# Layer 0's attention in 64-token chunks: a two-layer kernel on one core

## Chip, cores and metric

The kernel runs on one core of one Trainium2 chip, in one launch. The metric is the device time of an execution in microseconds (us); the median of several runs is compared. TensorE (PE in the profile) multiplies matrices into PSUM, with weight loads (PEld) beside it; VectorE (DVE), ScalarE (ACT) and GpSimd (POOL) work on elements; SyncE (SP) issues most DMAs.

## What is computed

The input is 16 sequences of 512 tokens with 128 features. Two layers follow, each as x + attention(norm(x)) + feed-forward(norm(x)). Cut to what matters:

```python
x  = L0_attn_x                                   # (16, 512, 128), float32
xn = layernorm(x)
x  = x + linear_attention(xn) + moe(xn)          # layer 0
xn = layernorm(x)
x  = x + softmax_attention_64(xn) + channel_mix(xn)   # layer 1

def linear_attention(x):                         # 16 heads of 8
    q, k, v = heads(x @ Wq.T), heads(x @ Wk.T), heads(x @ Wv.T)
    q, k = rope(q, k); q, k = elu(q) + 1, elu(k) + 1
    for each token t:                            # per head
        K_sum += k_t ; KV += outer(k_t, v_t)
        y_t = (q_t @ KV) / max(q_t . K_sum, 1e-6)
    return y @ Wo.T
```

`moe` sends each token to the 2 best of 8 experts (hidden size 512, squared ReLU) and adds a shared expert. Layer 1's softmax attention lets a query see all keys up to the end of its chunk of 64.

The change touches `linear_attention` alone. It is computed in chunks: the tokens of earlier chunks enter through a running state (KV and K_sum summed over them), those of the query's own chunk through masked scores, (q k^T where key <= query) times v. A column of ones beside v gives the denominators.

## The kernel before

**Recorder and scheduler.** The code records its operations instead of issuing them. `Program.call` (line 314) keeps each with an engine, an estimated cost and its tiles; for TensorE it also keeps a form, the rows and columns of the array that are used. `program.unit()` groups matmuls that are issued without a break. `Program.run` (line 409) then goes through them as a list scheduler: for each engine it takes, of what is ready, what was recorded first, and it emits every instruction. So all instructions carry the lines of the emitting helpers (L326; L331 for whole matmuls split into four strips of 32 columns, so that the array's shape stays; L514 for matmuls with constants that fill planned pauses of more than `IDLE`). One reads the profile by tiles. `TURN` (line 278) is what the scheduler reckons for a change of shape. Indirect DMAs on POOL are kept `SPACE` apart and tied to a matmul of that time.

**What sets the recorded order.** Four chains of generators: `dispatch` (norm, routing, sending tokens to their experts' slots by indirect DMAs), `slot_tiles` (the experts), `layer0`, `layer1`. The sequences form four groups of four; layer 0 of a group is recorded beside layer 1 of the group before. `PACE` (line 284) gives each chain its begin and its pace, one row for the first group, one for the middle ones, one for the last; `LAYER_STEPS` (line 108) is the number of steps for a sequence.

**Layer 0's attention**, for a sequence of NT = 4 tiles of P = 128 tokens:

- `linear_operands` (line 964) projects q, k, v, applies rope and phi (tile `qr`), and writes v into strips (`vpad`, `vstrips`). Then come the states: for each of the first three tiles a matmul of `qr` with `vstrips` adds to one accumulator in PSUM, and VectorE copies it, masked by head blocks (`blocks`), into a state tile. Each copy stands between two matmuls of the same accumulator. Then q and k are transposed to `qT`, `kT`, and ScalarE makes `q0m`: q four times, each with other heads zeroed.
- `linear_attention` (line 1055) goes through the tiles t. `scores(t)` is a unit of 8 matmuls (32 rows by 128 columns of the array, 256 moving columns) into two pairs of PSUM banks; VectorE masks both pairs with `causal` into `am` (two products of 128x1024). `weigh(t, ams, oT)` (line 1086) is a unit of 8 matmuls that read the state (`q0T,state`, from the second tile on) and 16 with the masked scores (`am,vpad`), all 128 rows by 32 columns with 128 moving columns, into one bank. ScalarE copies it to `oT`. After two tiles `finish` transposes back and divides.

Layer 1 shows in the profile as `qa,ka` (scores for maxima), `maxima` (VectorE), `ka,qa` (scores again, transposed), `ex` (ScalarE's exponential) and `ex,vpad` (weighted values).

Of the kernel before, what the change touches and what calls it, by code (L numbers as in the profile page):

```python
# [29 lines left out]
F32 = mybir.dt.float32  # L30
# [24 lines left out]
def slot_count(gt):  # L55
# [14 lines left out]

VPAD = (H - 1) * (PAIR + 2) + 32
# [17 lines left out]
    ("causal", P), ("rank", E), ("upper", P), ("ones", P), ("tile", SLOT_TILES),  # L89
# [18 lines left out]
LAYER_STEPS = (16, 40)  # L108
# [145 lines left out]
class Op:  # L254


    def __init__(self, engine, emit, cost, later, index):
        self.engine, self.emit, self.cost, self.later, self.index = engine, emit, cost, later, index
        self.needs, self.bases, self.wrote, self.then = set(), set(), set(), []
        self.missing, self.ready, self.result, self.done = 0, 0.0, None, False  # L260

        self.spaced = False

        self.form, self.strips, self.narrow = None, None, False
# [13 lines left out]
TURN = {(32, 128): 208, (128, 32): 138, (128, 128): 148}  # L278

SPACE = 1900  # L280

# [3 lines left out]
    (0.1, 0.4, 0.26, 0.8, 0.0, 0.8, 0.0, 1.23),  # L285
    (0.3, 0.4, 0.2, 0.8, -0.09, 1.0, 0.22, 1.0),
    (0.0, 0.58, 0.27, 0.76, 0.18, 1.0, 0.0, 1.0),
# [3 lines left out]
class Program:  # L291
# [22 lines left out]
    def call(self, name, api, method, args, kw):  # L314
# [18 lines left out]
        if name == "PE":  # L333
# [4 lines left out]
            elif args[1].shape[0] == 32:  # L338
                cost = max(0.425 * n, 56.0)
            elif o.shape[0] == 32:  # L340
                cost = max(0.425 * n, 56.0)
            else:
                cost = max(1.68 * n, 224.0)
# [16 lines left out]
        if name == "PE":  # L360
            (self.unit_of[0] if self.unit_of else op).form = form
# [47 lines left out]
    def run(self):  # L409
# [20 lines left out]
        while emitted < len(self.ops):  # L430
# [27 lines left out]
            if op.spaced:  # L458
                self.spaced_to = start + SPACE
# [6 lines left out]
            if name == "PE":  # L466
                if self.form != (P, P) and all(part.strips for part in op.parts or [op]):
                    op.form, op.narrow = (P, 32), True
                if op.form != self.form:
                    end += TURN.get(op.form, 148)  # L470
                    self.form = op.form
# [152 lines left out]
def two_layers(ctx: ExitStack, tc: tile.TileContext, x, small, const, w_fc, w_proj, out):  # L624
# [145 lines left out]
    for i in range(NT - 1):  # L770
        st = fixed.tile([P, 8, 32], F32, tag=f"state{i}", name=f"state{i}")
# [158 lines left out]
    def tokens_to_heads(o, name, tag):  # L930
# [11 lines left out]
        "vpad": 0, "qr": ("qr", 1), "T": ("q0T", "k0T", 1), "q0m": ("q0m", 2), "am": ("am", 2),  # L942
# [3 lines left out]
        "vpad": 2, "qr": ("ka", 2), "T": ("qa", "qa", 2), "q0m": ("probs", 4), "am": ("ka", 2),  # L946
# [3 lines left out]

    def lent_layer():

        a = p3.tile([P, 1024], F32, tag="probs", name="vstrips_lent", bufs=4)
        LENT["vstrips"] = a[:, 0 : NT * 8 * (PAIR + 2)].rearrange(
            "p (t s e) -> p t s e", t=NT, e=PAIR + 2
        )
        G.memset(a, 1.0)
        a = p3.tile([P, 1024], F32, tag="probs", name="states_lent", bufs=4)
        LENT["states"] = [
            a[:, i * 256 : (i + 1) * 256].rearrange("p (s e) -> p s e", e=32) for i in range(NT - 1)  # L960
        ]
        G.memset(a, 0.0)

    def linear_operands(xnT, b, home):
# [51 lines left out]
        pst = one(f"state_{b}")  # L1016
        for t in range(NT - 1):
            M.matmul(
                pst[:, 0 : 8 * (PAIR + 2)], qr[:, t, D : 2 * D],
                vs[:, t, :, :].rearrange("p s e -> p (s e)"),  # L1020
                start=(t == 0), stop=(t == NT - 2), skip_group_check=True,
            )
            V.tensor_tensor(
                states[t][:, :, 0 : PAIR + 2],
                pst[:, 0 : 8 * (PAIR + 2)].rearrange("p (s e) -> p s e", e=PAIR + 2), blocks,
                ALU.mult,
            )
# [13 lines left out]
        qT, kT = both  # L1041
        qms = []
        for u in range(2):
            tag, bufs = home["q0m"]
            qm = (p3 if tag == "probs" else p2).tile(
                [P, 2, T], F32, tag=tag, name=f"q0m_{b}_{u}", bufs=bufs
            )
            for o in range(2):
                r = 2 * u + o
                S.activation(qm[:, o, :], qT, AF.Copy, scale=c_("pick")[:, r : r + 1])  # L1050
            qms.append(qm)
# [3 lines left out]
    def linear_attention(operands, b, home):  # L1055
# [4 lines left out]
        def scores(t):  # L1060

            scs = [big(f"sc0_{b}_{t}_{pr}") for pr in range(2)]
            cols = slice(t * P, (t + 1) * P)
            with program.unit():
                for u in range(2):
                    for j in range(4):
                        rows = slice(32 * j, 32 * j + 32)
                        M.matmul(
                            scs[j // 2][:, j % 2, 2 * u * P : 2 * (u + 1) * P].rearrange(
                                "p (o q) -> p o q", o=2  # L1070
                            ),
                            kT[rows, cols], qms[u][rows, :, cols], start=True, stop=True,
                        )
            ams = []
            for pr, sc in enumerate(scs):
                tag, bufs = home["am"]
                am = p2.tile([P, 2, 512], F32, tag=tag, name=f"am_{b}_{t}_{pr}", bufs=bufs)
                V.tensor_tensor(
                    am.rearrange("p j (t q) -> p j t q", q=P),
                    sc.rearrange("p j (t q) -> p j t q", q=P),  # L1080
                    causal.unsqueeze(1).unsqueeze(1).to_broadcast([P, 2, NT, P]), ALU.mult,
# [4 lines left out]
        def weigh(t, ams, oT):  # L1086

            po = one(f"o0_{b}_{t}")

            with program.unit():  # L1090
                for u in range(2):
                    for j in range(4):
                        o = po[32 * j : 32 * j + 32, u * P : (u + 1) * P]
# [765 lines left out]
```

## Time and profile before

| | |
|---|---|
| runs shown | 1570.34, 1570.38, 1571.56 us, median 1570.38 |
| profiled execution | 1572.36 us; its span from first to last instruction 1570.6 us |
| granted TensorE clock | 0.997 |
| matmul records of TensorE | 23232 |
| layer 1's `maxima`, VectorE | 448 instructions, 385.7 us |
| layer 1's `ex`, ScalarE | 320 instructions, 311.5 us |
| layer 0's mask `am`, VectorE | 128 instructions, 151.0 us |
| layer 0's copies to `oTs`, ScalarE | 64 instructions of 128x256, 24.0 us |

A group's row reads: line, engine, operation, out<-in, shape, count, then busy time, mean duration of one in ns, and idle time of the engine just before, with what ended it. "32*128" ahead of a shape is the part of the array: rows by columns. Durations of matmuls overlap, so their sum is not time; the distance from one start to the next is. A row of the timeline reads: start, length from the first start to the last end, engine, line, operation, shape, count, and in brackets idle time before it.

### The profile page before, as it was taken

What the parts mean: (1) busy time and instruction counts of PE and PEld (TensorE: products, weight loads), DVE (VectorE), ACT (ScalarE), POOL (GpSimd) and SP (SyncE); (2) the same over time, 40 slices, a digit from 0 to 9 for tenths busy, and PEclk for the clock granted to TensorE, in tenths of its full rate; (3) what the DMA queues carried; (4) which work ended last, traced back from release to release, by engine and by line L of the source; (5) the groups of instructions that cost most, each with busy time, mean ns of one, the idle gap of its engine ahead of it and who ended that gap; (6) DMA issues with size and microseconds to landing.
All of it is one profiled execution on the core that took longest, in us unless ns stands there. A gap on an engine that the chain in (4) does not pass through costs nothing. (4 is left out here: it accounts for less than half of the span.)

```text
span 1570.6 us, 53937 instructions
## 1 busy us (share of the span) xinstructions
PE 1474.0 (94%) x23232; PEld 977.6 (62%) x23232; DVE 1064.1 (68%) x2289; ACT 865.0 (55%) x1369; POOL 392.3 (25%) x425
## 2 busy tenths in 40 slices
PE   6899998999999999999999999999999989998887
PEld 5678887766666657666666666566666555444444
DVE  6864431787876777588685767586757786765763
ACT  3336464565655555655656566655665545455444
POOL 3540142342035241114400140200000521442220
PEclk9999999999999999999999999999999999999999
DMA  6247687554244554334241434431321100000000
GB/s 191 89 132 233 188 245 224 161 159 146 83 141 128 146 145 133 99 110 137 83 136 36 141 98 124 119 89 53 108 85 42 39 27 15 22 15 8 8 2 14
DMA packets 150238, 163.09 MB, mean 104 GB/s; under 512 B 12912, under 2 KB 97648, under 8 KB 150000
## 3 DMA queue, kind: packets, MB, share of 16 engines
q1 hardware_dynamic: 141808, 142.86, 30.8%
q0 software_dynamic: 8192, 16.79, 3.6%
q8 instruction: 182, 2.98, 0.8%
q14 instruction: 56, 0.46, 0.1%
HBM read 118.71 MB, written 40.89 MB: 102 GB/s over the span
## 5 line engine op out<-in xcount | busy, mean ns | idle before, releaser
L326 DVE TENSOR_REDUCE maxima<-banks 128x2 f32<-128x768 f32 (+2 forms) x448 | 385.7, 914 | 82.1 <-PE banks L326 77.2
L326 ACT ACTIVATE ex<-banks 128x1024 f32<-128x1024 f32 x320 | 311.5, 1021 | 137.7 <-PE banks L326 130.1
L326 DVE TENSOR_TENSOR am<-banks,const_sb 128x1024 f32<-128x1024 f32 x128 | 151.0, 1220 | 122.1 <-PE banks L326 118.3
L326 PE MATMUL banks<-qa,ka 32*128 32x512 f32 (+3 forms) x2048 | 194.1, 460 | 14.5 <-ACT ex L326 6.3
L1223 POOL DMA_INDIRECT rows<-xn,pl_slot x128 | 128.1, 1000 | 304.5 <-DVE pl_slot L326 173.4
L326 PE MATMUL banks<-ka,qa 32*128 32x512 f32 (+2 forms) x1792 | 185.0, 503 | 17.5 <-ACT ex L326 10.9
L1242 POOL DMA_INDIRECT back<-results,pl_slot x128 | 128.1, 1001 | 290.2 <-PE banks L326 184.0
L326 PE MATMUL banks<-ex,vpad 128*32 128x512 f32 (+3 forms) x2048 | 173.1, 439 | 0.9 <-issue 0.5
L326 PEld LDWEIGHTS banks<-qa,ka 32*128 32x128 f32 x2048 | 95.8, 183 | 91.3 <-ACT ex L326 25.6
L326 ACT ACTIVATE hg<-banks 128x512 f32<-128x512 f32 x156 | 92.9, 597 | 103.6 <-PE banks L331 80.1
L326 PEld LDWEIGHTS banks<-ka,qa 32*128 32x128 f32 x1792 | 80.4, 184 | 79.5 <-issue 20.1
L331 PE MATMUL banks<-wp,hg 128*32 128x128 f32 x3104 | 104.9, 274 | 10.2 <-issue 6.0
L326 PEld LDWEIGHTS banks<-ex,vpad 128*32 128x32 f32 x2048 | 52.6, 109 | 91.4 <-issue 64.3
L331 PE MATMUL banks<-xgT,wf 128*32 128x128 f32 x3104 | 106.0, 274 | 3.3 <-issue 1.6
L331 PEld LDWEIGHTS banks<-wp,hg 128*32 128x32 f32 x3104 | 87.5, 110 | 34.5 <-issue 21.1
L331 PEld LDWEIGHTS banks<-xgT,wf 128*32 128x32 f32 x3104 | 85.9, 110 | 27.6 <-issue 11.5
L326 ACT COPY oTs<-banks 128x256 f32<-128x256 f32 (+1 forms) x96 | 42.8, 445 | 98.7 <-PE banks L326 93.8
L326 PE MATMUL banks<-am,vpad 128*32 128x128 f32 x2048 | 82.2, 274 | 4.5 <-issue 2.0
L326 ACT ACTIVATE hg<-hg 128x1024 f32<-128x1024 f32 x80 | 83.0, 1038 | 2.5
L326 PE MATMUL banks<-q0m,k0T 32*128 32x256 f32 x1024 | 74.6, 400 | 2.3 <-ACT ex L326 1.0
L326 ACT COPY yg<-banks 128x256 f32<-128x256 f32 x80 | 29.3, 367 | 83.6 <-PE banks L331 60.4
L326 PEld LDWEIGHTS banks<-am,vpad 128*32 128x32 f32 x2048 | 59.2, 110 | 15.5 <-issue 8.3
(226 smaller groups left out, 2343.9 us busy)
## 6 DMA issues: line engine op xcount, KB each, us to landing
wf<-in_w_fc SPq DMA_DIRECT2D x156, 256.0 KB
wp<-in_w_proj SPq DMA_DIRECT2D x156, 256.0 KB
rows<-zeros SPq DMA_DIRECT2D x4, 2496.0 KB
results<-yg SPq DMA_DIRECT2D x76, 128.0 KB
xg<-rows SPq DMA_DIRECT2D x36, 256.0 KB
x_in<-in_x SPq DMA_DIRECT2D x16, 256.0 KB
x<-x SPq DMA_DIRECT2D x16, 256.0 KB
out<-rr SPq DMA_DIRECT2D x16, 256.0 KB
```

The lines of the kernel that those rows point to most:

```text
L326: return getattr(api, method)(*map(made, args), **{k: made(a) for k, a in kw.items()})
L331: yield api.matmul(to[at : at + 32], weights[:, at : at + 32], *rest, **kw)
L1223: i = nc.gpsimd.indirect_dma_start(out=rows.made()[:, :], out_offset=bass.IndirectOffsetOnAxis(ap=slot.made(), axis=0), in_=row.made(), in ...
L1242: "POOL", lambda: nc.gpsimd.indirect_dma_start(out=o.made(), out_offset=None, in_=results.made()[:, :], in_offset=bass.IndirectOffsetOnAxi ...
```

## The change

Chunks become CH = 64 tokens, so there are eight chunks and seven states. The steps now go by pairs of tiles (tp), two for a sequence. `scores(tp)` is one unit of 16 matmuls (32 rows by 64 columns, 256 moving columns; for the one sequence with borrowed buffers 32 of 128), two masks instead of four for a pair. `weigh(tp)` is one unit: 24 or 32 state reads (32 by 32) and 64 products with masked scores (64 by 32), all of 64 moving columns, into two banks, and one ScalarE copy. The states come from one unit of seven matmuls (64 rows), two masked copies, and six sums on VectorE. `LAYER_STEPS`, `PACE` and the scheduler's estimates of costs and turns change with it. The constants `SPACE_FIRST` and `SPACE` are equal.

```diff
+CH = P // 2
+CHUNKS = T // CH
+STATE_N = 8 * (PAIR + 2) + 16
...
-    ("causal", P), ("rank", E), ("upper", P), ("ones", P), ("tile", SLOT_TILES),
+    ("causal", CH), ("rank", E), ("upper", P), ("ones", P), ("tile", SLOT_TILES),
...
-LAYER_STEPS = (16, 40)
+LAYER_STEPS = (12, 40)
...
-TURN = {(32, 128): 208, (128, 32): 138, (128, 128): 148}
+TURN = {(32, 128): 208, (32, CH): 208, (128, 32): 138, (CH, 32): 138, (128, 128): 148}
+SPACE_FIRST = 1900
...
-    (0.1, 0.4, 0.26, 0.8, 0.0, 0.8, 0.0, 1.23),
-    (0.3, 0.4, 0.2, 0.8, -0.09, 1.0, 0.22, 1.0),
-    (0.0, 0.58, 0.27, 0.76, 0.18, 1.0, 0.0, 1.0),
+    (0.1, 0.4, 0.31, 0.68, 0.0, 0.58, 0.01, 1.28),
+    (0.3, 0.41, 0.12, 0.8, -0.26, 1.0, 0.25, 1.0),
+    (-0.27, 0.45, 0.41, 0.66, 0.05, 0.94, 0.2, 0.89),
...
-            elif args[1].shape[0] == 32:
-                cost = max(0.425 * n, 56.0)
-            elif o.shape[0] == 32:
-                cost = max(0.425 * n, 56.0)
+            elif form[0] == CH and form[1] == P:
+                cost = 0.84 * n
+            elif form[0] == 32 and form[1] > 32:
+                cost = max(0.425 * n * o.shape[0] / P, 28.0)
+            elif form[1] == 32:
+                cost = max(0.425 * n, 28.0)
...
-        pst = one(f"state_{b}")
-        for t in range(NT - 1):
-            M.matmul(
-                pst[:, 0 : 8 * (PAIR + 2)], qr[:, t, D : 2 * D],
-                vs[:, t, :, :].rearrange("p s e -> p (s e)"),
-                start=(t == 0), stop=(t == NT - 2), skip_group_check=True,
-            )
-            V.tensor_tensor(
-                states[t][:, :, 0 : PAIR + 2],
-                pst[:, 0 : 8 * (PAIR + 2)].rearrange("p (s e) -> p s e", e=PAIR + 2), blocks,
-                ALU.mult,
-            )
+        n = 8 * (PAIR + 2)
+        pst, last = big(f"state_{b}"), one(f"state_last_{b}")
+        with program.unit():
+            for i in range(CHUNKS - 1):
+                t, c = i // 2, i % 2
+                rows = slice(c * CH, (c + 1) * CH)
+                M.matmul(
+                    pst[:, c, t * n : (t + 1) * n] if i < CHUNKS - 2 else last[:, 0:n],
+                    qr[rows, t, D : 2 * D], vs[rows, t, :, :].rearrange("p s e -> p (s e)"),
+                    start=True, stop=True, skip_group_check=True,
+                )
+        V.tensor_tensor(
+            states[0][:, :, 0:n].rearrange("p (t c) e -> p c t e", c=2),
+            pst[:, :, 0 : 3 * n].rearrange("p c (t e) -> p c t e", t=3),
+            c_("blocks").unsqueeze(1).unsqueeze(1).to_broadcast([P, 2, 3, n]), ALU.mult,
+        )
+        V.tensor_tensor(states[1][:, 0, 0:n], last[:, 0:n], c_("blocks"), ALU.mult)
+        for i in range(1, CHUNKS - 1):
+            upto = state_of(states, i)[:, 0:n]
+            V.tensor_tensor(upto, upto, state_of(states, i - 1)[:, 0:n], ALU.add)
...
+        def parts(tp):
+            for t in (2 * tp, 2 * tp + 1):
+                for c in range(2):
+                    yield t, c, slice(c * CH, (c + 1) * CH), slice(t * P + c * CH, t * P + (c + 1) * CH)
...
-        def scores(t):
+        def scores(tp):
...
+                for r, n, qm in qms:
+                    for t, c, half, cols in parts(tp):
+                        at = (t % 2) * 4 * CH + r * CH
+                        for j in range(4):
+                            rows = slice(32 * j, 32 * j + 32)
+                            M.matmul(
+                                scs[j // 2][half, j % 2, at : at + n * CH].rearrange(
+                                    "p (o q) -> p o q", q=CH
+                                ),
+                                kT[rows, cols], qm[rows, :, cols], start=True, stop=True,
+                            )
...
-        def weigh(t, ams, oT):
-            po = one(f"o0_{b}_{t}")
+        def weigh(tp, ams, oT):
+            po, begun = big(f"o0_{b}_{tp}"), set()
...
+                for t, c, _, cols in parts(tp):
+                    for u in range(2):
+                        for j in range(4):
+                            if 2 * t + c:
+                                o, kw = to(t, c, u, j)
+                                at = (4 * u + j) * (PAIR + 2)
+                                rows = slice(32 * j, 32 * j + 32)
+                                M.matmul(
+                                    o, state_of(states, 2 * t + c - 1)[rows, at : at + 32],
+                                    qT[rows, cols], stop=False, **kw,
+                                )
+                for t in (2 * tp, 2 * tp + 1):
+                    for u in range(2):
+                        for o_ in range(2):
+                            for j in range(4):
+                                for c in range(2):
+                                    half = slice(c * CH, (c + 1) * CH)
+                                    o, kw = to(t, c, u, j)
+                                    at = (t % 2) * 4 * CH + (2 * u + o_) * CH
+                                    M.matmul(
+                                        o, strip(vp, t, 8 * u + 2 * j + o_)[half, :],
+                                        ams[j // 2][half, j % 2, at : at + CH],
+                                        stop=(o_ == 1), **kw,
+                                    )
-            S.copy(oT[:, (t % 2) * 2 * P : (t % 2 + 1) * 2 * P], po[:, 0 : 2 * P])
+            S.copy(
+                oT.rearrange("p (n c q) -> p n c q", c=2, q=CH),
+                po[:, :, 0 : 4 * CH].rearrange("p c (n q) -> p c n q", q=CH),
+            )
...
-        i.spaced = True
+        i.spaced = SPACE_FIRST if sent is not None and len(rows_in) == 0 and not routed else SPACE
```

`to(t, c, u, j)` is the place of the result: partitions 32j to 32j+31 of bank c, 64 columns at (2 (t mod 2) + u) 64.

## The prediction

> **What bounds the kernel now.** I read four views: the page's busy times, the busy times by stretch, the groups of instructions, and the timeline of TensorE. First the page and three stretches. I cut them where the trace shows layer 1's first product with the probabilities (`ex,vpad`, 328 us) and layer 0's last product with the masked scores (`am,vpad`, 1335 us).
>
> ```profile
> PE 1474.0 (94%) x23232; PEld 977.6 (62%) x23232; DVE 1064.1 (68%) x2289; ACT 865.0 (55%) x1369; POOL 392.3 (25%) x425
> 0.00:328.00 328.00, 295.63 (x4549) 236.19 (x4549) 179.29 (x467) 159.76 (x292) 107.45 (x133) 0.99 0.60 180
> 328.00:1335.00 1007.00, 975.49 (x16360) 633.05 (x16363) 735.92 (x1524) 592.21 (x929) 219.49 (x239) 1.00 0.34 101
> 1335.00:1571.00 236.00, 202.92 (x2331) 108.34 (x2322) 148.88 (x300) 113.01 (x150) 65.33 (x55) 0.99 0.04 11
> ```
>
> After the length come PE, PEld, DVE, ACT and POOL, then granted clock, DMA share and GB/s. In the 1007 us in the middle TensorE is busy 97% of the time at full clock, VectorE 73%, the DMA engines a third. So in the stretch that holds most of layer 0, TensorE's stream sets the time, and what it no longer streams is gained. The last 236 us are layer 1 alone.
>
> Next the groups that the change touches, then TensorE's timeline, where durations overlap and only distances between starts are a price.
>
> ```profile
> L326 PE MATMUL banks<-am,vpad 128*32 128x128 f32 x2048 | 82.2, 274 | 4.5 <-issue 2.0 <-DVE am L326 1.6 <-DVE maxima L326 0.5
> L326 PE MATMUL banks<-q0m,k0T 32*128 32x256 f32 x1024 | 74.6, 400 | 2.3 <-ACT ex L326 1.0 <-issue 0.6 <-DVE maxima L326 0.6
> L326 DVE TENSOR_TENSOR am<-banks,const_sb 128x1024 f32<-128x1024 f32 x128 | 151.0, 1220 | 122.1 <-PE banks L326 118.3 <-ACT ex L326 2.6 <-ACT h L326 0.8
> L326 DVE TENSOR_TENSOR state<-banks,const_sb 128x144 f32<-128x144 f32 x45 | 13.7, 304 | 20.2 <-PE banks L326 15.3 <-PE banks L331 3.1 <-issue 1.0
> L326 DVE TENSOR_TENSOR pl_sum<-pl_sum 128x128 f32<-128x128 f32 x16 | 4.7, 291 | 0.5
> ```
> ```profile
> 67.96 0.40 PE L326 MATMUL banks<-q0T,state 128*32 128x128 f32 x8
> 68.18 0.42 PE L326 MATMUL banks<-am,vpad 128*32 128x128 f32 x6
> 68.92 0.43 PE L326 MATMUL banks<-am,vpad 128*32 128x128 f32 x5 [0.32 <-issue]
> 69.68 0.44 PE L326 MATMUL banks<-am,vpad 128*32 128x128 f32 x5 [0.32 <-issue]
> 70.04 1.15 PE L326 MATMUL banks<-q0m,k0T 32*128 32x256 f32 x16
> ...
> 616.85 0.46 PE L331 MATMUL banks<-small_sb,xnT 128*32 128x8 f32 x32
> 617.24 1.14 PE L326 MATMUL banks<-qa,ka 32*128 32x512 f32 x8
> ...
> 709.22 0.40 PE L326 MATMUL banks<-q0T,state 128*32 128x128 f32 x8
> 709.43 0.62 PE L326 MATMUL banks<-am,vpad 128*32 128x128 f32 x16
> ...
> 747.74 1.15 PE L326 MATMUL banks<-q0m,k0T 32*128 32x256 f32 x16
> 748.82 1.07 PE L326 MATMUL banks<-ex,vpad 128*32 128x256 f32 x16
> ```
>
> `128*32` is the part of the array used: 128 rows (the contraction) by 32 columns. A float32 matmul has two records (1024 `am,vpad` matmuls are built, 2048 recorded). From 709.22 to 709.43, eight records of 128 columns on four tiles side by side take 0.218 us, by neighbouring starts too: a pass of 128 columns is 109 ns, shared by four tiles. From 747.74 to 748.82, sixteen records of 256 columns take 1.08 us: 0.87 of stream at that rate and 0.21 for changing the array's shape. The 32 records of 8 columns at 616.85 are not streaming but issue: 0.46 us less one duration of 0.18 us, so a start each 8.8 ns, its weight load included. At 68.18 the sixteen records that should take 0.44 us take 1.86: an "issue" stall, 1.4 us lost. TensorE's waits list 45 gaps of this kind, 16.3 us.
>
> **The change, part by part.** The built order gives the counts: 12,078 matmuls before, 13,387 after. All prices are 109 ns a pass of 128 columns, two passes a matmul, divided by the tiles side by side.
>
> Removed, all 16 sequences. Scores: 512 matmuls of 256 columns on four tiles, 109 ns each, 55.8 us. Products with the masked scores: 1024 of 128 columns, 54.5 ns, 55.8. State reads: 384, 20.9. State updates: 22 whole ones of 144 columns at 245 ns and 104 strips at 61, 11.8. Together 144.3 us.
>
> Added. Scores: 480 of 256 columns and 64 of 128, on 32x64 tiles, eight of which fit the array: 54.5 and 27 ns, 27.9 us. State updates: 112 of 144 columns, two side by side, 122.6 ns, 13.7. State reads: 896 of 64 columns on four diagonal 32x32 tiles, 27.2 ns, 24.4. Masked products: 2048 of 64 columns on 64x32 tiles. No row shows eight tiles in this form. The low end is streaming, 54.5 ns for a pass of eight, 27.9 us; the high end is only four at once, 55.8. I take issue as the limit, since the 8-column burst is the nearest row: 8 x 8.8 = 70 ns for a pass of eight, 35.8 us. Together 101.8, a gain of 42.5.
>
> Changes of shape: 838 before, 841 after, hence nothing (0.8 us from the different mix, counted at 0.21 us into a shape of 32 rows and 0.14 to 0.15 into the others). Elsewhere, other products stand whole or in strips in another mix and there are ten more filling matmuls: +2.1. TensorE's stream: -42.5 + 0.8 + 2.1 = -40 us.
>
> [...]
>
> VectorE: masks go from 128 to 64 of the same size, 64 x 1.22 = -78 us. States: 48 x 0.304 = 14.6 removed; added for each sequence one product of 864 elements (1.05 us, between 0.691 for 512 and 1.22 for 1024), one of 144 (0.30) and six sums (0.29 each, by `pl_sum`), 3.1 x 16 = 50. Net -43 us. On an engine at 73% beside TensorE at 97% this is hidden; it pays only where TensorE waited for it (`am` 2.7 us, `maxima` 14.8): -3. The six sums stand in line before the first read of a state, 2.7 us after the update; the scores and two masks (2.4 us) are ahead of that read anyway, and if uncovered it costs at most 1 us for each sequence, as other units are ready. ScalarE: 64 copies at 0.375 become 32 at 0.587, -5 us, hidden. SP's queue has as many entries as before, POOL one memset less; the spacing of POOL's indirect DMAs keeps its 1900, so their queues only follow TensorE.
>
> Order. The begins and paces are new, and the built order shows their effect: before layer 1's first `ex,vpad` stand six sequences' masked products (five before), and after layer 0's last there are 5.4 sequences' `ex,vpad` (4.25 before). So 1.1 sequences more of layer 1 run alone. Pricing the built streams as above, the tail had 192 us of stream in 236 us, 44 lost on 4.25 sequences, 10.4 each: +12. The middle had 943 of stream in 1007, 6.8% lost; it now has some 90 us less stream: -6. Together +6.
>
> Stalls at issue. Each weighing unit now has 88 or 96 short matmuls, with loads 352 or 384 instructions, as fast as 4.4 ns each; 64 in a row is the longest such burst that the trace has. Of the 64 old weighing units 4 stalled (seven of the gaps stand before an `am,vpad`); with four times the density I take one in four of the 32 new ones, 8 x 1.4 = +11 (ends: none, and all, +45).
>
> Sum: -40 - 3 + 6 + 11 = -26 us. The profiled span is 1570.6 (its run's own time 1572.4); the median of the runs is 1570.38, the span within 0.02%, so I take the difference off it: **1544 us**.
>
> **Rivals.** First, the two halves of the rows do not run together in the masked products. For it: no row has both row and column parts. Against: row parts alone (`q0m,k0T`) and column parts alone (`am,vpad`) each run four at once. Price +20, with some 6 us less of stalls: 1558.
> Second, no stalls at all and streaming the limit: 8 off the stream and 11 off the stalls, 1525. For it: six of the eight 8-column bursts ran through.
> Third, slower: instruction supply becomes the bound of the weighing units. The longer runs of narrow products never went faster than 16 instructions in 218 ns, 13.6 ns each. If TensorE cannot be fed faster for long, the 2944 short matmuls, 11,776 instructions, take 160 us in place of 60: 1544 - 11 + 100 = 1633. It decides from 8.2 ns an instruction, where 97 us would eat up the 37 that remain without stalls. Two of the eight bursts, which broke off after 22 and 26 records, speak for it; that the old runs were paced by their columns speaks against.
> Fourth, the change is made but the order gives all back, no change: a middle bound by layer 1's own chain. The 86 us a sequence in the middle (1007 over 11.75) against 55 alone (236 over 4.25) speaks against.
>
> **How the numbers follow.** Forecast 0.40, second 0.24, first 0.22, slower 0.10, no change 0.04. A measurement of this kernel can tell some 0.2% from nothing. All but the last two are faster: 0.86, 0.04, 0.10. Range: from below the second case (1525, its order term uncertain by one sequence, 10 us) to above the first (1558, the same): 1517 to 1567. The slower case stays outside.
>
> **What would show it.** In the changed profile: starts of `am,vpad` some 9 ns apart in eights with 55 to 70 ns from one eight to the next (right), or in fours with 55 (first rival); `q0m,k0T` units of 16 matmuls in about 1.1 us; the masks 64 times at 1.22; "issue" before TensorE below 35 us; `ex,vpad` alone for some 290 us at the end. Wrong: weighing units beyond 3 us, or TensorE's idle in the middle up by more than 30 us.

## The result, and the profile after

The changed kernel is slower: 1596.88 us in the median (1591.32 to 1599.50, four runs) against 1570.36 for the kernel before on the same chip, a ratio of 1.0159 [1.0141, 1.0177]. The profiled span went from 1570.6 to 1597.7 us, +27.1. (In the diff above, the `oT` side of ScalarE's copy should read `p (n c q) -> p c n q`, like the side of `po` below it.)

The busy times of the page, and the instruction queue among its DMA queues:

```profile
PE 1462.7 (92%) x25850; PEld 966.3 (60%) x25850; DVE 1024.4 (64%) x2305; ACT 857.1 (54%) x1337; POOL 387.9 (24%) x424
q8 instruction: 203, 3.33, 0.9%
```

TensorE is less busy than before by 11 us and yet the span is longer. Its instructions arrived in 203 packets of 16,384 bytes (182 before). 25,850 matmul records and as many weight loads over 203 packets are 255 instructions a packet (255 before too), so I take a packet for a block of 256 instructions; in `f4` below they come 256 at a time. A float32 matmul, with two records and two loads, is four instructions.

The busy times by stretch, cut at the same two events as before (first `ex,vpad`, now at 376 us; last `am,vpad`, at 1305):

```profile
0.00:376.00 376.00, 318.61 (x5937) 249.93 (x5937) 180.63 (x483) 160.58 (x292) 106.58 (x129) 0.94 0.54 160
376.00:1305.00 929.00, 891.09 (x16993) 581.99 (x16989) 653.95 (x1438) 555.79 (x862) 193.82 (x217) 1.00 0.37 107
1305.00:1597.00 292.00, 252.95 (x2931) 134.33 (x2924) 189.83 (x384) 140.73 (x185) 87.49 (x78) 1.00 0.05 14
```

The middle is 78 us shorter (some 96 were priced) and the tail 56 longer (as priced). The first stretch, into which a sixth sequence's products moved, is 48 us longer; only 23 of these are more busy time of TensorE, and the clock fell from 0.99 to 0.94 there.

The groups that the change touched:

```profile
L334 PE MATMUL banks<-am,vpad 64*32 64x64 f32 x4096 | 58.2, 236 | 21.0 <-issue 20.6
...
L334 DVE TENSOR_TENSOR am<-banks,const_sb 128x1024 f32<-128x1024 f32 x64 | 75.6, 1218 | 62.9 <-PE banks L334 61.6
```

TensorE's waits that the profile puts down to nothing but issue, with total, number and longest:

```profile
PE banks L334 <- issue: 37.3, 60, 2.8
PE banks L339 <- issue: 20.9, 36, 2.4
```

These are 58.2 us where the two rows of before had 16.3. Two stretches of TensorE's timeline show what happens, the first two sequences' weighing units and a lone unit later:

```profile
66.94 1.23 PE L334 MATMUL banks<-q0T,state 32*32 32x64 f32 x48
68.09 0.30 PE L334 MATMUL banks<-am,vpad 64*32 64x64 f32 x3
68.63 1.46 PE L334 MATMUL banks<-am,vpad 64*32 64x64 f32 x125 [0.24 <-issue]
70.02 0.65 PE L334 MATMUL banks<-q0T,states_lent 32*32 32x64 f32 x32
72.46 0.43 PE L334 MATMUL banks<-q0T,states_lent 32*32 32x64 f32 x16 [1.79 <-issue]
72.82 2.14 PE L334 MATMUL banks<-am,vpad 64*32 64x64 f32 x112
76.19 0.47 PE L334 MATMUL banks<-am,vpad 64*32 64x64 f32 x16 [1.23 <-issue]
...
717.57 1.10 PE L334 MATMUL banks<-q0T,state 32*32 32x64 f32 x64
718.59 1.48 PE L334 MATMUL banks<-am,vpad 64*32 64x64 f32 x128
```

The lone unit runs through in 2.44 us (717.57 to 720.01 by starts). Its first products start 6 to 7 ns apart in eights, and all 128 of their records come 10 ns apart in the mean, 80 ns for eight, where four at a time would need 109: eight tiles do run side by side. The two units in a row stand still twice for over 1 us, after 32 of 48 and after 112 of 128 records, with nothing to wait for. Taken from a unit's first start to the next start of other work, all weighing units together took 125.8 us, against 93.7 before. At the two clean values that occur (2.22 us with 88 matmuls, 2.44 with 96) they would take 74.6, and only seven of the 32 units show them. So 51 us were lost inside these units. In the kernel before, whose clean values are 0.90 or 1.01 us (16 matmuls) and 1.33 or 1.45 (24), by what follows, the same count gives 83.1 clean and 10.6 lost. The waits list only 31 us of idle time for the units after; in the rest, records come through too densely to leave a listed gap, but more slowly than in a clean unit, in part at half clock.

### The profile page after: what moved, and what is told of

It reads as the page before. It is cut to its first block, busy times and chain, and to the rows that moved or that the text cites. A ratio compares the mean times of both kernels' runs of the same rounds, so it can differ in the third digit from the quotient of the medians.

```text
span 1597.7 us, 59152 instructions
## 1 busy us (share of the span) xinstructions
PE 1462.7 (92%) x25850; PEld 966.3 (60%) x25850; DVE 1024.4 (64%) x2305; ACT 857.1 (54%) x1337; POOL 387.9 (24%) x424
## 3 DMA queue, kind: packets, MB, share of 16 engines
q1 hardware_dynamic: 141808, 142.82, 30.4%
## 4 chain that ended last, share of the span: by engine, by line
PE 41%; DVE 7%; ACT 4%; issue 2%; DMA 1%; DVEq 0%; ACTq 0%
PE banks L334 31%; PE banks L339 10%; DVE maxima L334 5%; ACT ex L334 3%; DMA x<-x 0%; DVE rr L334 0%; DMA out<-rr 0%; DVE by_cos L334 0%; DVE gf_z L334 0%; ACT h L334 0%; ACT hg L334 0%; DVE qa L334 0%; DVE x L334 0%; PE banks L528 0%; ACT xr L334 0%
## 5 line engine op out<-in xcount | busy, mean ns | idle before, releaser
L334 PE MATMUL banks<-qa,ka 32*128 32x512 f32 (+3 forms) x2048 | 190.0, 459 | 15.3 <-ACT ex L334 8.1
L334 PEld LDWEIGHTS banks<-qa,ka 32*128 32x128 f32 x2048 | 93.5, 183 | 85.7 <-ACT ex L334 25.8
L339 PE MATMUL banks<-xgT,wf 128*32 128x128 f32 x3072 | 107.7, 278 | 10.6 <-issue 9.2
L334 DVE TENSOR_TENSOR am<-banks,const_sb 128x1024 f32<-128x1024 f32 x64 | 75.6, 1218 | 62.9 <-PE banks L334 61.6
L339 PEld LDWEIGHTS banks<-xgT,wf 128*32 128x32 f32 x3072 | 86.8, 111 | 41.9 <-issue 26.3
L334 PEld LDWEIGHTS banks<-ex,vpad 128*32 128x32 f32 x2048 | 51.2, 109 | 95.2 <-issue 64.4
L334 ACT COPY oTs<-banks 128x512 f32<-128x512 f32 x64 | 37.5, 586 | 121.6 <-PE banks L334 116.4
L339 PE MATMUL banks<-wp,hg 128*32 128x128 f32 x2592 | 88.8, 275 | 10.7 <-issue 6.9
L339 PEld LDWEIGHTS banks<-wp,hg 128*32 128x32 f32 x2592 | 73.2, 110 | 30.5 <-issue 19.7
L334 PE MATMUL banks<-am,vpad 64*32 64x64 f32 x4096 | 58.2, 236 | 21.0 <-issue 20.6
L334 PE MATMUL banks<-wp,hg 128*128 128x128 f32 x600 | 74.9, 277 | 2.4 <-ACT hg L334 2.2
L334 PEld LDWEIGHTS banks<-wp,hg 128*128 128x128 f32 x600 | 70.1, 192 | 6.3 <-ACT hg L334 4.3
```

The lines of the kernel that those rows point to most:

```text
L334: return getattr(api, method)(*map(made, args), **{k: made(a) for k, a in kw.items()})
L339: yield api.matmul(to[at : at + 32], weights[:, at : at + 32], *rest, **kw)
```

## The experiments

There were eighteen runs in five sets, each set on one chip with the kernel before beside it. The kernel before itself took 1531.8, 1531.7, 1570.9, 1533.7 and 1570.4 us in the five sets, so sets differ by 2.5% and only ratios are compared across sets. Whether that is the chip is not shown: the first and the third set are both recorded as chip number 7. "Issue idle" is the sum of TensorE's waits for issue, as above. The expectations name times of the result's own set, about 1570 us for the kernel before; for the sets at 1532 read them as ratios.

### First set: plan, strips or chunks

Four edits. `e1`: the changed kernel with the `PACE` rows of before. `e4`: the kernel before with the new rows.

```diff
 PACE = (
-    (0.1, 0.4, 0.31, 0.68, 0.0, 0.58, 0.01, 1.28),
+    (0.1, 0.4, 0.26, 0.8, 0.0, 0.8, 0.0, 1.23),
...
```

`e2` and `e3`: the kernel after and the kernel before without the cutting of whole matmuls into four strips (L339 and L331).

```diff
-            op.strips = strips if method == "matmul" and form == (P, P) else None
+            op.strips = None
```

> The changed kernel with the old three rows of PACE; chunks, tiles and costs stay. Supply theory (TensorE's short matmuls are taken faster than its instructions come, and every stall at 'issue' holds the only busy engine): the instructions stay, so the time stays near 1597 us (1585 to 1605), with over 45 us of issue gaps before PE. Order theory (the new begins and paces let layer 1 start at 376 us instead of 328, and give back what the chunks gain): some 1550 us, with the first ex,vpad back near 330.

> The changed kernel, with no 128x128 matmul split into four strips: 9741 matmuls instead of 13387, 876 changes of shape instead of 841, the same arithmetic. Supply theory: a quarter fewer instructions leave room beside the weighing units, issue gaps fall from 58 us to below 25, and the time falls to 1555 or less. Order theory and a theory that the short tiles are slow in themselves: no gain, and up to 6 us lost to 35 more changes of shape, 1595 to 1605.

> The kernel before with no 128x128 matmul split into strips: 8111 matmuls instead of 12078, 896 changes of shape instead of 838. Supply theory: it had 16 us of issue gaps to lose, and 58 more changes of shape cost some 8 us: 1558 to 1572. Rival (strips are worth much by themselves): 1580 or more.

> The kernel before with the new three rows of PACE (LAYER_STEPS stays 16). Order theory: it loses what the changed kernel loses, 1590 or more. Supply theory: within 10 us of 1570.

| run | ratio to before | issue idle, us | weighing units, us |
|---|---|---|---|
| e1, chunks, old plan | 1.0251 [1.0222, 1.0281] | 42.8 | 120.0 |
| e2, chunks, no strips | 1.0170 [1.0148, 1.0192] | 30.4 | 110.4 |
| e3, before, no strips | 1.0142 [1.0125, 1.0159] | 0 | 88.1 |
| e4, before, new plan | 1.0071 [1.0045, 1.0097] | 1.9 | 88.3 |

The new plan alone is not the cause: with it the old kernel loses 11 us, about the 10 that the supply theory allowed, where the order theory asked for 20, and without it the chunks lose more, more even than either theory had. `e2` and `e3` both missed what the supply theory expected (ratios of at most 0.990 and 1.001 on the basis of 1570 us) and came out where its rivals had put them, because strips are worth more than was thought, 1.4% to the old kernel. So the two must be read against each other: without strips on either side, the chunks lose only 5.0 us (1558.53 against 1553.52), though they still stall for 30 us, 25 of them at weighing units, where the old kernel does not stall at all. Strips use four times the instructions for the same work; beside the chunks they seem worth less (1.0170 without, 1.0138 with them in the next set, intervals that overlap).

### Second set: the supply by itself

`f1` and `f2` are the two kernels once more. `f3` cuts the weighing unit into three, the later two ranked behind other work, so that matmuls of long rows may come between:

```diff
-            with program.unit():
-                ... state reads, products of both tiles
+            apart(0, (reads, t0), (reads, t1))
+            apart(1, (products, t0, 0), (products, t0, 1))
+            apart(2, (products, t1, 0), (products, t1, 1))
```

`f4` is a kernel of TensorE bursts, the first with this loop:

```python
for n in (48, 96, 144, 192, 256):
    pause(14)          # 14 matmuls of 128x128 by 512 columns
    short(n, 64)       # n products 64x32 by 64 columns, as in a weighing unit
```

> The changed kernel once more, to have its trace beside the others of one chip. Supply theory (TensorE's instructions come in blocks of 256 that land no closer together than about 3.3 us, at most two blocks ahead, and a weighing unit of 88 or 96 matmuls of 64x64 uses 352 or 384 of them in some 2.4 us): as before, 1.012 to 1.020 times the kernel before, idle time of TensorE put down to issue 50 to 60 us, weighing units together 120 to 126 us. Order theory (the fitted begin and pace are what costs): the same time, so this run alone doesn't tell them apart; it is the base line of the split.

> The kernel before once more, for its trace on this chip. Supply theory: idle time of TensorE put down to issue under 20 us, and that at line 331 and 326 in the densest stretches, where 256 instructions go in 3.4 us. Order theory: no forecast.

> The weighing unit is cut into three (state reads, products of the first tile, products of the second), the later two ranked behind other work so that matmuls of long rows come between. Supply theory: the same products now fit into what has been fetched, so the time from the start of each such run of matmuls to the next thing on TensorE adds up to 90 to 105 us in place of about 123, issue idle falls from 50 to 60 us to 25 to 35, and the ratio to the kernel before falls by 0.010 to 0.020, to 0.995 to 1.008; what the two more changes of tile per unit cost (20 more, some 3 us) is in that. Theory of slow tiles (64x64 products take some 3.6 us in themselves, however spread): sum 120 or more, ratio 1.015 to 1.022. Order theory: the order hardly changes, ratio 1.015 to 1.02.

> Nothing of the layers is computed: TensorE alone, bursts of 48, 96, 144, 192, 256 and 1024 of the 64x64 products (64 columns), then 512 of 128x32 with 64 columns, 512 with 128 and 256 with 192, each behind 14 matmuls of 128x512 that take some 12 us and use few instructions. Each matmul is four instructions in the trace (two passes, a weight load and a matmul each). Supply theory: 48 and 96 go at 25 to 28 ns each (1.3 and 2.5 us); from 128 on (512 instructions) each further 64 cost 3.3 us, so 256 take 9 to 10 us and 1024 some 47 to 50 us; 512 of 128x32 with 64 columns take 24 to 27 us and 512 with 128 columns (106 ns by the eviction-free rate of 0.425 ns a column for two passes) 50 to 55 us, without stalls. Theory of slow tiles or of a limit at issue alone: the time goes up evenly, 1024 take 26 to 36 us at one pace, with no step at 128.

TensorE's timeline in `f4`: L28 are the pauses, L34 the short products (two records each), L43 narrow ones of 128x32.

```profile
20.77 1.17 PE L34 MATMUL banks<-w 64*32 64x64 f32 x96
21.86 12.28 PE L28 MATMUL banks<-w 128*128 128x512 f32 x28
34.08 2.02 PE L34 MATMUL banks<-w 64*32 64x64 f32 x183
38.81 0.32 PE L34 MATMUL banks<-w 64*32 64x64 f32 x9 [2.71 <-issue]
...
115.91 2.47 PE L34 MATMUL banks<-w 64*32 64x64 f32 x231
120.15 1.47 PE L34 MATMUL banks<-w 64*32 64x64 f32 x128 [1.77 <-issue]
124.15 2.04 PE L34 MATMUL banks<-w 64*32 64x64 f32 x128 [2.53 <-issue]
128.16 2.04 PE L34 MATMUL banks<-w 64*32 64x64 f32 x128 [1.96 <-issue]
131.61 2.04 PE L34 MATMUL banks<-w 64*32 64x64 f32 x128 [1.42 <-issue]
```
```profile
186.73 3.09 PE L43 MATMUL banks<-w 128*32 128x64 f32 x203
191.10 1.99 PE L43 MATMUL banks<-w 128*32 128x64 f32 x128 [1.28 <-issue]
194.83 1.99 PE L43 MATMUL banks<-w 128*32 128x64 f32 x128 [1.74 <-issue]
...
226.81 28.15 PE L43 MATMUL banks<-w 128*32 128x128 f32 x1024
```

This is the mechanism laid bare. 48 products take 1.10 us, 22.9 ns each. Behind 12 us of pause, in which a few dozen instructions are used, the long burst gets 231 records far, 462 instructions, and then stops. The other bursts that stall stop after 159 to 259 records, 318 to 518 instructions: some two blocks of 256 at most are ready, and where in a block a burst begins seems to decide how many instructions. Even 96 products, as many matmuls as a weighing unit, stopped at the 183rd of their 192 records (34.08). From there on exactly 128 records and their 128 loads, one block, come at a time, each about 3.45 us after the last at best (128.16, 131.61, 135.06) and 3.71 in the mean of the burst, though the block is used up in 1.3 to 1.8 us; 1024 products took 56.7 us, 55 ns each. With 128x32 tiles it is the same (512 in 27.9 us), so it is not the small tile. Nor is it the clock: it stood at 0.5 from 121.8 to 176.4 us, through most of the long burst, but at 1.0 in the burst of 128x32 tiles until 210.6, whose blocks came 3.7 us apart. With 128 columns (226.81) there is no stall: 54.9 ns each, 64 of them 3.5 us, just the pace of the supply. The trace of the blocks' queue shows why they are so far apart: in this burst a fetch starts only 1.0 to 1.7 us after TensorE has resumed, takes 0.9 to 1.5, and the records resume 1.2 to 1.5 us after it is in. No two overlap. The steps came as the supply theory had them; its time for 1024 (47 to 50 us) was too low, and its 50 to 55 us for 512 with 128 columns, which charged 106 ns a matmul where 54.9 were measured, was nearly double the 28.2 measured.

| run | ratio to before | issue idle, us | weighing units, us |
|---|---|---|---|
| f1, after | 1.0138 [1.0116, 1.0160] | 46.2 | 118.4 |
| f2, before | (1.0) | 1.9 | 89.6 |
| f3, unit in three | 1.0074 [1.0049, 1.0098] | 32.7 | 112.5 |

In `f1` each of the 35 gaps at issue ends 1.0 to 1.7 us after a block has landed (1.2 to 1.5 in `f4`): on this set the stalls at issue are all of this kind. Splitting takes back nearly half of the loss, without changing what is multiplied. That speaks for the supply and against slow tiles, but the sum over the units fell only to 112.5 where 90 to 105 were expected: often nothing with long rows came between, and two parts still follow each other or meet a half-used block, as here in `f3`'s timeline, where 124 of 128 records pass and four wait:

```profile
717.60 1.45 PE L336 MATMUL banks<-am,vpad 64*32 64x64 f32 x124
720.42 0.30 PE L336 MATMUL banks<-am,vpad 64*32 64x64 f32 x4 [1.37 <-issue]
```

### Third set: fewer products, and a plan that knows

`g1` leaves out the masked products of every second head, so its time is that of a kernel with 1024 fewer matmuls: `for o_ in range(1)` in place of `range(2)`. `g2` gives the short matmuls 56 ns in the scheduler's costs in place of 28. `g3` lets the scheduler keep an account of fetched instructions, and `g4` joins that with the split:

```diff
+                left -= uses                      # four for each matmul
+                end += max(0.0, -left) * BLOCK / 256          # BLOCK = 3450 ns
...
+    def _left(self, t):
+        return min(512.0, self.stock + max(0.0, t - self.stocked) * 256 / BLOCK)
```

> Left out: the masked products of every second head (1024 of the 2048 of 64x32), so a weighing unit has 56 or 64 matmuls, 224 or 256 instructions, in place of 352 or 384. In the runs alone the products went at 19.4 ns each when nothing was missing (64 in 1.24 us), so leaving out 1024 is worth 20 us where every instruction is at hand. Supply theory: it is worth more, since most of what the units stalled goes too: issue idle from 46 to 12 to 25 us, weighing units from 118 to 60 to 72 us, 40 to 55 us off the whole, ratio 0.978 to 0.988. Theory of slow tiles or order: 20 us off, some 27 if each kept its share of today's pace (118 us over 2944 matmuls is 40 ns each, so 41 us off the units, if the pace is the tiles' own: then issue idle stays near 46), ratio 0.995 to 1.002.

> The planner reckons each short matmul at 56 ns again, as in the kernel before, in place of 28: its times come closer to what the runs alone kept up (55 ns each), the instructions are the same to 21 matmuls. Supply theory: a plan can't make instructions come faster, so issue idle stays at 38 to 50 us; only what comes due beside the units fits better, ratio 1.008 to 1.018. Order theory (the plan's error about these units is what costs): most of the loss goes, ratio 0.990 to 1.003.

> The planner keeps an account of fetched instructions (512 at most, 256 more each 3.45 us, four to a matmul): a unit that needs more than is there lets another ready one with few instructions go first, the cut of a whole matmul into four is left out where the account is low, and the end of a unit that overdraws it comes later. Supply theory: the stalls are filled with work that is there anyway, issue idle 25 to 38 us and ratio 0.998 to 1.010. Order theory: like the plan with 56 ns.

> The weighing unit cut into three and the account of fetched instructions together. Supply theory: what splitting alone left (32.7 us issue idle, ratio 1.0074) falls further, to 15 to 28 us idle and a ratio of 0.992 to 1.004, less than that if the 31 more changes of tile (some 5 us) and 303 more matmuls eat it. Theory of slow tiles: no better than 1.012.

| run | ratio to before | issue idle, us | weighing units, us |
|---|---|---|---|
| g1, half the products | 0.9843 [0.9823, 0.9864] | 25.8 | 79.0 |
| g2, plan at 56 ns | 1.0340 [1.0311, 1.0370] | 65.8 | 149.2 |
| g3, plan with supply | 1.0156 [1.0132, 1.0179] | 51.4 | 129.0 |
| g4, both | 1.0131 [1.0112, 1.0150] | 46.7 | 126.4 |

`g1` gives 3.2% of 1570, 50 us, for products that cost 20 us when their instructions are at hand. The other 30 us are stalls that went with them, as the supply theory had it in the ratio (issue idle from 58 to 26, units of 79 us; both a little above its ranges). Of the 26 us only 3.8 still end 1.0 to 1.7 us after a block's landing, 32.4 in the changed kernel. The three plans missed. A plan that charges the pace of a long burst (`g2`) makes it worse: its units take 149 us and the clock falls to 0.971 in the mean; why this order stalls so much more wasn't tested. An account in the scheduler (`g3`) doesn't help. It was too kind, perhaps: it lets a block come in each 3.45 us at any moment, whereas in `f4` a fetch starts only 1.0 to 1.7 us after TensorE has resumed, and the blocks came 3.71 us apart in the mean. That wasn't tested either. `g4` may gain something over the changed kernel (its ratio of 1.0131 stands beside 1.0159), less than expected.

### Fourth set: instructions alone, and where

This set tells the count from all else. `h1` is the kernel before in which each matmul of a weighing unit is two of half the columns: same tiles, same operands, same columns in all, and the same order (the cost that the scheduler reckons for a unit is kept).

```diff
+                        for h in range(0, P, 64):
+                            at, c = u * P + h, (2 * u + o_) * P + h
                             for j in range(4):
                                 M.matmul(
-                                    po[32 * j : 32 * j + 32, u * P : (u + 1) * P],
-                                    strip(...), ams[j // 2][:, j % 2, c : c + P],
+                                    po[32 * j : 32 * j + 32, at : at + 64],
+                                    strip(...), ams[j // 2][:, j % 2, c : c + 64],
```

`h2` keeps the old form for the first eight sequences (`b < 8`) and the chunks for the last eight, `h3` does so with the old `PACE` rows for the first and the middle groups, and `h4` splits the late weighing units as `f3` did.

> The kernel before, in which every matmul of the weighing units (128x32, 128 columns) is two of 64 columns: the same tiles, columns, operands and order, 1408 matmuls more (13,486 against 12,078, about as many as the changed kernel's 13,387), a unit of 48 matmuls or 192 instructions for the same 1.45 us at 28 ns each. Supply theory (256 instructions each 3.45 us): 15 to 45 us slower, ratio 1.010 to 1.029, issue idle up by 15 to 40 us, and units that take 2 to 4 us. Any theory in which the chunks' own tiles, their order or plan cost: no change, ratio 0.998 to 1.003, issue idle as before.

> The first eight sequences have their attention in the form of before (tiles of 128), the last eight in chunks of 64, all with the new begin and pace. Supply theory: the stalls of the first 400 us go (32 of the 58 us of issue idle), and half of what the chunks save is kept: issue idle 20 to 32 us, ratio 1.000 to 1.010. Theory of the plan (new begin and pace cost): ratio 1.007 or more, as the kernel before had with this plan.

> As the run before, with the begin and pace of before for the first two groups of sequences. Supply theory: the first half is then the kernel before; behind it half of the saving of 26 us against some 15 to 20 us of stalls: ratio 0.994 to 1.004, issue idle 20 to 32 us. Theory of the plan: as the run before less some 0.007.

> As the run before, and the weighing units of the late sequences cut into three. Supply theory: 5 to 8 us less than the run before, ratio 0.989 to 1.000, issue idle 12 to 24 us. Theory of slow tiles or of the plan: the same as the run before.

| run | ratio to before | issue idle, us | weighing units, us |
|---|---|---|---|
| h1, before, twice the instructions | 1.0132 [1.0103, 1.0160] | 14.1 | 101.6 |
| h2, late chunks, new plan | 1.0028 [1.0008, 1.0048] | 15.4 | 95.5 |
| h3, late chunks, old plan in front | 1.0118 [1.0094, 1.0142] | 21.4 | 102.1 |
| h4, as h3, split | 1.0053 [1.0037, 1.0069] | 12.7 | 95.5 |

`h1` does nothing new and is 1.3% slower, about as much as the whole change in such a set. In `f2` (before, traced on the chip of the second set, 1532 us as here) and then in `h1`, the groups of the products and of the experts' first strips:

```profile
L326 PE MATMUL banks<-am,vpad 128*32 128x128 f32 x2048 | 78.9, 273 | 2.8 <-DVE am L326 1.6 <-issue 0.6 <-DVE maxima L326 0.5
...
L331 PE MATMUL banks<-xgT,wf 128*32 128x128 f32 x3104 | 103.0, 274 | 2.0 <-issue 1.1 <-ACT ex L326 0.6 <-DVE xs L326 0.4
```
```profile
L326 PE MATMUL banks<-am,vpad 128*32 128x64 f32 x4096 | 82.8, 220 | 10.5 <-issue 8.2 <-DVE am L326 1.8 <-DVE maxima L326 0.5
...
L331 PE MATMUL banks<-xgT,wf 128*32 128x128 f32 x3104 | 106.1, 276 | 4.2 <-issue 3.2 <-ACT ex L326 0.6 <-DVE xs L326 0.4
```

Since the order is the same, group stands against group. By distances from start to start, TensorE's work is 20.9 us longer: 12.0 in the weighing units, 4.5 in the strips of `xgT,wf`, 2.8 in `qa,ka`, 2.6 in three other strip groups, and no other group moved by over 0.6. It is not a price of each matmul: clean units take 1.48 us with 48 matmuls where they took 1.45 with 24, and most units are clean; the 12.0 us are lost in the units that stall, up to 3.95 us long. So units that outrun the supply also starve other dense work. Each of the 15 gaps at issue ends 1.0 to 1.7 us after a block's landing. Issue idle rose by 12 us, less than the 15 expected; of the rest at most 3.5 us is the clock (at 0.5 for 17.0 us, 10.0 in `f2`), and the remainder is time in which records come late but without a listed gap.

`h2` shows the place: with the chunks out of the dense front, the loss is 0.3%, in its range (the idle of 15.4 us is under it). `h3` missed; I expected the old plan to be better for the old half, and it is worse with this mix. `h4` is better than `h3` by 10 us, more than the 5 to 8 expected of the split, though its ratio stayed above the range named.

### Fifth set: a version that beats both?

`i1` is `h2` with the late units split, `i2` the same with chunks in the last four sequences only.

> Chunks in the last eight sequences, new begin and pace, and their weighing units cut into three. Supply theory: issue idle falls from 15 to 6 to 11 us and the ratio by 0.004 to 0.009 from 1.0028, to 0.994 to 0.999, which would beat both kernels. If what is left is the plan or the tail: 1.000 to 1.005.

> The same with chunks in the last four sequences alone. Supply theory: half of the chunks' saving and half of their stalls: issue idle 3 to 7 us, ratio 0.997 to 1.004, between the run beside it and the 1.0071 that the kernel before had with this plan. If the plan is what is left: 1.005 to 1.008.

They came out at 1.0082 [1.0069, 1.0095] and 1.0100 [1.0084, 1.0115], issue idle 31.0 and 24.8 us. Both miss. In this set the kernel before took 1570 us, as where its trace has 16 us of issue idle, and `h2` was not run in such a set. Only 10.4 and 6.1 us of the two sums end 1.0 to 1.7 us after a block's landing, about what the supply theory expected; the rest are gaps of the other kind described below. Why the ratios stay so high is not settled. No version here beats the kernel before.

## Why the prediction was wrong

The step that failed is "Stalls at issue": one in four of the 32 weighing units, 1.4 us each, +11. Measured, 25 of the 32 units took longer than a clean one, and together they lost 51.2 us, where the old units lost 10.6: +40.6. Issue idle elsewhere rose by 13 (27.4 us of it in the changed kernel outside these units, 14.3 before). The prediction took a stall for an accident that hits some units. `f4` shows a rate: four instructions a matmul, 352 or 384 in a unit, and 256 more only each 3.45 us at best in that burst. By that, a unit that meets two full blocks runs through, and one that begins in a half-used block, or follows another unit, stops.

Blocks are not all of it. The gaps at issue are of two kinds. In the sets where the kernel before takes some 1532 us, 210 of 213 end 1.0 to 1.7 us after a block has landed. In those where it takes 1570, the result's own among them, there are 37 to 90 more in each traced run, most of 0.3 to 0.4 us, that follow no such landing:

| issue idle, us | before | after |
|---|---|---|
| ending 1.0 to 1.7 us after a block's landing | 3.4 | 32.4 |
| others | 12.9 | 25.7 |

So most of the rise is the blocks. What makes the short gaps, and why they are found in these sets alone, is open; the change costs 1.4% without them (`f1`).

By terms, as distances from start to start on TensorE, the sum of all groups rose by 27.3 us:

| term | predicted | measured |
|---|---|---|
| scores | -27.9 | -31.5 |
| weighing, clean | -16.5 | -8.5 (74.6 for 83.1) |
| weighing, lost in the units | +11 | +40.6 (51.2 for 10.6) |
| state updates | +1.9 | +2.6 |
| all else (mix, shapes, waits, order) | +5.9 | +24.1 |

- **The stream.** The terms of the scores and of the updates were right to 4 us. Clean weighing saved half of its term: units of 74.6 us where the stream alone was priced at 60.2, since the products take 80 ns for eight records (70 priced) and each unit also pays for its changes of tile (in the lone unit 144 ns from the last state read to the first product and 145 from the last product to the next work, where starts inside it are at most 60 apart). Eight tiles do run at once; starts 6 to 7 ns apart in eights were what the forecast asked for (9 expected).
- **VectorE.** 1064.1 to 1024.4, -40 for -43 forecast; the masks are 64 of 1.218 us. TensorE's idle time ended by VectorE fell from 38.3 to 35.3, the -3 of the sum.
- **Order.** 5.375 sequences of layer 1 alone took 293 us, 54.5 each, for 55 each forecast. Moved to the kernel before, the plan costs 11 us (`e4`), for +6 here.
- **All else** is 18 us off. Of it 13 are issue idle outside the weighing units, as `h1` showed in small. Another part is the clock: it stood at 0.5 for 9 us before and 50 after, 44 of these in the first 330 us. By an estimate, 41 us more at half clock lose at most some 20 us of work, but a part of that falls into the weighing units and the stalls; how much is left was not separated.

**The rivals.** The first (no eights) and the second (no stalls) are refuted, the fourth too. The third, given 0.10, named the mechanism, "instruction supply becomes the bound of the weighing units", and its rate of 13.6 ns an instruction was near the 13.5 of the supply in `f4` (3.45 us over 256). It was dismissed because those runs were paced by their columns. They were: four tiles of 128 columns need 13.6 ns an instruction for their columns alone, which hides that the supply gives no more. Its price of 1633 was too high, as it charged the slow rate to every instruction, where up to two blocks are ready after a lull (up to 518 instructions in `f4`); its threshold of 8.2 ns was passed: 125.8 us over 11,776 instructions are 10.7. The stall already visible (sixteen records in 1.86 us at 68.18) was no sign of it: one block landed at 64.9 us and the next at 72.1, and TensorE resumed twice between them, so it is of the other kind. Fetched blocks could have been counted, though: 182 in 1570 us are one each 8.6 us, and 3.4 us at the closest, while a weighing unit of 2.4 us uses 1.5 blocks.

## What to carry to other kernels

Count TensorE's instructions, not only its columns: price a dense stretch at the larger of its stream and its supply, here 13.5 to 14.5 ns an instruction (54 to 58 ns for a float32 matmul) once the blocks at hand, 320 to 520 instructions in `f4`, are used. Cutting matmuls into smaller ones was not free here: `h1`, which does only that, ran at 1.0132. With other work let in between the parts of a unit (`f3`), nearly half of the chunks' loss came back (1.0074 for 1.0138). Two such savings (strips and chunks) seem to draw on the same store: without strips on either side the chunks lost only 5.0 us. To test such a suspicion cheaply, cut the old kernel's matmuls in two and leave all else alone.

## What the runs showed of the hardware

- The clock: in the changed kernel the granted clock falls to 0.5 eleven times before the end, for 3.4 or 6.8 us each, and in `f4`'s long burst for 54.6. In the 6.8 us before each of the eleven TensorE was idle for only 0.9 to 3.8 us, mostly in pieces; what sets the length is not shown.
- One program took 1531 or 1570 us, by the set. Of 39 us by starts on TensorE between the two traces, some 30 lie in strips and weighing units, and issue idle was 1.9 and 16.3 us, nearly all of the difference in short gaps that follow no block's landing. Blocks came no closer than 3.24 us (`e2`, a set at 1532) and 3.25 us (`g2`, at 1570); why some sets have these gaps is open.
